# A selective-scan block between two FP4 FFNs: all four channel chunks interleaved in the scan's tiles, and GpSimd making one of four B·du tiles

## The chip, the cores and the metric

The kernel runs on one core of one Trainium2 chip. The metric is the device time of one execution in microseconds (us); shorter is better. A core has five engines that each work through their own instruction queue in order: TensorE (PE: matmuls and transposes; PEld is its weight load), VectorE (DVE), ScalarE (ACT), GpSimd (POOL, which here also issues the accumulating DMAs) and SyncE (SP, which issues the other DMAs). [...] All arithmetic of this kernel is in f32.

## The reference, cut to what matters

The input is 8 sequences of 1024 tokens with 256 features. It passes through `x + 0.5 FFN(norm(x))`, then `x + Mamba(norm(x))`, then the same FFN again. Each FFN quantizes its activations and weights to FP4 in blocks of 16 and multiplies by 256x704, 256x704 and 704x256 matrices. The part that the change touches is the selective scan: 512 channels d, 16 states n, and for each batch a recurrence over the tokens t.

```python
dA = jnp.exp(delta[..., None] * A[None, None])
dBu = delta[..., None] * Bm[:, :, None, :] * u[..., None]
def step(h, inp):
    dA_t, dBu_t, c_t = inp
    h = dA_t * h + dBu_t
    y = jnp.einsum('bdn,bn->bd', h, c_t)
...
y = y + u * D_param          # then  y * silu(z) @ out_proj_w
```

## The kernel before

The 8192 tokens are cut into 16 chunks of 512 tokens (two per sequence). Every chunk s passes through five generators, `stage_f1` (first FFN), `stage_m1` (in-projection, convolution, x-projection, delta, du), `stage_z` (the gate), `scan` and `stage_out` (gate product, out-projection, second FFN). A table of due times at the end of the kernel lets the generators of several chunks emit their instructions interleaved, so that while chunk s is scanned, its neighbours' FFNs and projections run on the same engines.

For the scan the 512 channels are four channel chunks dc of 128 partitions, and the tokens lie along the free dimension. For each of the 16 states k, `scan_step` does four things:

- ACT multiplies `duT` (tokens on partitions, four token tiles t of 128 tokens by 512 channels) by the column of B for state k, which is one scalar per partition: four tiles `s_bu` of 128x512 (line 874). Line 872 could give some of them to DVE, but `BE` is zero, so all are ACT's. There are 7 buffers for these tiles.
- PE transposes each `s_bu` tile in four 128x128 blocks into the PSUM tile `s_pb`, so that channels are on partitions again (line 881). There are two `s_pb` buffers.
- ACT makes `s_da = exp(A delta)`, 128x512, for each dc (line 878).
- DVE runs the recurrence, one scan of 512 tokens for each dc (line 883), from `s_da` and `s_pb` into the tile `h`.

A tile `h` holds one state of all 512 channels, 2048 values on each of 128 partitions, in 5 buffers that are shared with `m_ud` and some prologue tiles. Its layout is `pairs`: two halves a, in each the tokens t, and at each token the two channel chunks q of the pair lie side by side. So a scan writes every second value, and half a is complete after the second of its two scans. `times_c` (line 888) then multiplies each half by the row of C on GpSimd, 1024 values with each value of C used for two neighbours. ACT copies the last token's state to `s_carry` when the sequence has a second chunk (line 908); the multiplication overwrites `h`, so the second half waits for this copy too. Then GpSimd issues one DMA that adds the whole tile to one of two accumulators `accd` in HBM (line 920); SP stores the first one of the odd states (line 918), and `stage_m1` stores u·D there first (`m_ud`, lines 802 to 804). After the last state two more DMAs bring both accumulators back into `h` (lines 914, 915), and `stage_out` multiplies with the gate `m_sz`, again on GpSimd, in two halves (line 852). In the last chunk (s = 15) DVE takes part in the last two multiplications and in the sum.

The order of the instructions on each engine is not the order of the program. `set_order` builds the graph of all instructions, prices each by `price` (lines 141 to 177), plans forwards and backwards many times, plays the best plans with random delays and pins the best order for each engine. The prices that matter here are for GpSimd:

```python
if kind == "InstTensorTensor":
    step, inner = dims(ins[1])[-1]
    return n * (2.106 if step else 1.64 + 0.47 / inner) + (165 if n > 16 else 145), 0, 0, port
if kind == "InstTensorScalarPtr":
    slow = sum(size(a) == 1 for a in ins) > 1
    return (n * 4 + 190 if slow else n + 330), 0, 0, port
```

Whatever changes an instruction or its price therefore changes the order on all engines. GpSimd has other work that is ordered around the scan: the scale and the two block-wise multiplications of the FP4 quantization (lines 543, 545, 552), two small operations of each layer norm (610, 613), and delta·u (803).

Of the kernel before, what the change touches and what calls it, by code (L numbers as in the profile page):

```python
# [11 lines left out]
F32 = mybir.dt.float32  # L12
BF16 = mybir.dt.bfloat16
I32 = mybir.dt.int32
AF = mybir.ActivationFunctionType
ALU = mybir.AluOpType
# [5 lines left out]
P = 128  # L22
T = 512
# [14 lines left out]
KS = 1  # L38
KE = 1
W_T = ((0.01, 0.08, 0.085), (0.02, 0.09, 0.095), (0.15, 0.25, 0.3), 0.2)  # L40

BE = (0,)
CE = (0,)
BUFS = {
    'accd': 4, 'bcol': 2, 'big': 1, 'bu': 7, 'carry': 2, 'cbc': 2, 'cd': 4, 'da': 4, 'delta': 2,
# [17 lines left out]
ND = DI // P  # L63
# [364 lines left out]
def macaron(ctx: ExitStack, tc: tile.TileContext, x_in, norm_w, norm_b, in_w, conv_w,  # L428
            conv_b, xp_w, dt_w, dt_b, a_log, d_par, out_w, w_gate, w_up, w_down, out):
    nc = tc.nc  # L430
    NB, L, _ = x_in.shape
    chunks = []
    for b in range(NB):
        t = 0
# [3 lines left out]
    S = len(chunks)  # L438

    const = ctx.enter_context(tc.tile_pool(name="const", bufs=1))  # L440
    sb = ctx.enter_context(tc.tile_pool(name="sb", bufs=2))
# [16 lines left out]
    dr = ctx.enter_context(tc.tile_pool(name="dr", bufs=3, space=DRAM))  # L458
    sb, psq, psb, dr = Pool(sb), Pool(psq), Pool(psb), Pool(dr)
    pools = [Pool(q) for q in pools]  # L460

    def pst(shape, name):
        turn[kind[0]] += 1
        i = PSM[kind[0]][turn[kind[0]] % len(PSM[kind[0]])]
        t = pools[i].tile([P, 512], F32, tag=f"ps{i}", name=name)
        n = 1
        for k in shape[1:]:
            n *= k
        v = t[: shape[0], :n]
        if len(shape) == 3:  # L470
            v = v.rearrange("p (a b) -> p a b", a=shape[1])
        return v
# [14 lines left out]
    def cload(shape, src, name):  # L487
        t = const.tile(shape, F32, name=name)
        loads.append((t, src))
        return t  # L490
# [3 lines left out]
    def eng(what):  # L494
        return getattr(nc, ENG[what])
# [15 lines left out]
    dh = cload([P, ND], d_par.rearrange("(c p) -> p c", p=P), "dh")  # L511
# [14 lines left out]
        nc.vector.tensor_scalar(an, an, -1.0, None, ALU.mult)  # L526
        yield

    def pairs(h, n):

        return h.rearrange("p (a t q) -> p a t q", a=ND // 2, q=2)[:, :, :n, :]


    def quant(v, n, floor, mul0, mul1):
# [162 lines left out]
    x1d, accd, szd, cd = {}, {}, {}, {}  # L697
    duT, delta, bcol = {}, {}, {}
    carry = {}
# [3 lines left out]
    def tok(ap, s):  # L703
        b, t0, n = chunks[s]
        return ap[b, t0 : t0 + n, :].rearrange("(t p) d -> p t d", p=P)
# [11 lines left out]
    def stage_m1(s):  # L717
        n = chunks[s][2]
        nt = n // P
# [14 lines left out]
        for pr in range(nt // 2):  # L734
# [4 lines left out]
            for j in range(2):  # L739
                t = 2 * pr + j  # L740
                b, r = stats[t]
# [8 lines left out]
        u2 = sb.tile([P, ND, T], F32, tag="big", bufs=BUFS["big"], name="m_u2")  # L750
# [29 lines left out]
        pb = pst([P, nt, P], "m_pb")  # L780
# [12 lines left out]
        nc.scalar.activation(dl, dl, AF.Softplus)  # L793
        yield

        accd[s] = dr.tile([2, P, ND // 2, 2 * T], F32, tag="accd", bufs=BUFS["accd"], name="accd")
        ud = pairs(sb.tile([P, ND * T], F32, tag="h", bufs=BUFS["h"], name="m_ud"), n)
        dg = 1 if fine else DG
        for d0 in range(0, ND, dg):
            d1 = slice(d0, d0 + dg)  # L800
            for dc in range(d0, d0 + dg):
                nc.scalar.activation(ud[:, dc // 2, :, dc % 2], u2[:, dc, :n], AF.Copy, scale=dh[:, dc : dc + 1])
            eng('du').tensor_tensor(u2[:, d1, :n], u2[:, d1, :n], dl[:, d1], ALU.mult)
        nc.sync.dma_start(accd[s][0], ud.rearrange("p a t q -> p a (t q)"))
        yield
        duT[s] = []
        for t in range(nt):
# [22 lines left out]
    y_of, last_h = {}, {}  # L830

    def load_y(s):
        y = pairs(sb.tile([P, ND * T], F32, tag="big", bufs=BUFS["big"], name="o_y"), chunks[s][2])
        yf = y.rearrange("p a t q -> p a (t q)")
        nc.sync.dma_start(yf, accd[s][0])
        nc.gpsimd.dma_start(yf, accd[s][1], accum_op=ALU.add)
        return y

    def stage_out(s):
        n = chunks[s][2]  # L840
        nt = n // P
        muls = (eng('hx'), eng('hq')) if s < S - ENDV else (nc.vector, nc.vector)
        x4 = sb.tile([P, NT, DM], F32, tag="x4", bufs=BUFS["x4"], name="x4b")
        nc.sync.dma_start(x4[:, :nt], x1d[s][:, :nt])
        y, sz = y_of.pop(s), szd[s]

        for a in range(ND // 2):
            if s in last_h:
                for h in last_h[s]:
                    nc.vector.tensor_tensor(y[:, a], y[:, a], h[:, a], ALU.add)  # L850
            zv = sz[:, 2 * a : 2 * a + 2, :]
            (eng('y') if s < S - KE else nc.vector).tensor_tensor(zv, y[:, a].rearrange("p t q -> p q t"), zv, ALU.mult)
        yield
        for t in range(nt):
            po = pst([P, DM], "o_po")
            for dc in range(ND):
                nc.tensor.matmul(po, sz[:, dc, t * P : (t + 1) * P], outw[:, dc, :], start=(dc == 0), stop=(dc == ND - 1))  # L857
            nc.vector.tensor_tensor(x4[:, t, :], x4[:, t, :], po, ALU.add)
        yield
        yield from ffn(x4, nt, muls, s >= S - KE)  # L860
        nc.sync.dma_start(tok(out, s), x4[:, :nt])

    def scan_step(s, k, h):
        n = chunks[s][2]
        nt = n // P
        first = chunks[s][1] == 0
        bu_v = BE[S - 1 - s] if S - 1 - s < len(BE) else 0
        bu = []
        for t in range(nt):
            b = sb.tile([P, DI], F32, tag="bu", bufs=BUFS["bu"], name="s_bu")  # L870
            if t * bu_v % nt < bu_v:
                nc.vector.tensor_scalar(b, duT[s][t], bcol[s][:, t, k : k + 1], None, ALU.mult)
            else:
                nc.scalar.activation(b, duT[s][t], AF.Copy, scale=bcol[s][:, t, k : k + 1])  # L874
            bu.append(b)
        for dc in range(ND):
            da = sb.tile([P, T], F32, tag="da", bufs=BUFS["da"], name="s_da")[:, :n]
            nc.scalar.activation(da, delta[s][dc], AF.Exp, scale=an[:, dc, k : k + 1])  # L878
            pb = psb.tile([P, T], F32, tag="psb", name="s_pb")[:, :n]
            for t in range(nt):  # L880
                nc.tensor.transpose(pb[:, t * P : (t + 1) * P], bu[t][:, dc * P : (dc + 1) * P], ident)  # L881
            init = 0.0 if first else carry[chunks[s][0]][:, k, dc : dc + 1]
            nc.vector.tensor_tensor_scan(h[:, dc // 2, :, dc % 2], da, pb, init, ALU.mult, ALU.add)  # L883

    def times_c(s, k, h, cbc):
        last = s >= S - KE and k >= NS - 2
        for a in range(ND // 2):
            (nc.vector if last and a else nc.gpsimd).tensor_tensor(  # L888
                h[:, a], h[:, a], cbc.unsqueeze(2).to_broadcast([P, chunks[s][2], 2]), ALU.mult)

    def scan(s):
        n = chunks[s][2]
        if chunks[s][1] == 0:

            carry[chunks[s][0]] = sb.tile([P, NS, ND], F32, tag="carry", bufs=BUFS["carry"], name="s_carry")
        for k in range(0, NS, 2):
            cbc = sb.tile([P, 2, T], F32, tag="cbc", bufs=BUFS["cbc"], name="s_cbc")[:, :, :n]
            nc.sync.dma_start(cbc, cd[s][0:1, k * n : (k + 2) * n].rearrange("o (a t) -> o a t", a=2)
                              .partition_broadcast(P))
            if s >= S - KE and k == NS - 2:  # L900
                y_of[s] = load_y(s)
            last = s >= S - KE and k == NS - 2
            for j in range(2):
                h = pairs(sb.tile([P, ND * T], F32, tag="h", bufs=BUFS["h"], name="s_h"), n)
                hf = h.rearrange("p a t q -> p a (t q)")
                scan_step(s, k + j, h)
                if chunks[s][1] + n < L:
                    nc.scalar.activation(carry[chunks[s][0]][:, k + j].rearrange("p (a q) -> p a q", q=2), h[:, :, n - 1, :], AF.Copy)  # L908
                times_c(s, k + j, h, cbc[:, j, :])
                if last:  # L910
                    last_h.setdefault(s, []).append(h)
                elif k + j == NS - 1:

                    nc.gpsimd.dma_start(hf, accd[s][1], accum_op=ALU.add)
                    nc.gpsimd.dma_start(hf, accd[s][0], accum_op=ALU.add)
                    y_of[s] = h
                elif k + j == 1:
                    nc.sync.dma_start(accd[s][1], hf)
                else:
                    nc.gpsimd.dma_start(accd[s][j], hf, accum_op=ALU.add)  # L920
                yield


# [55 lines left out]
```

## Time and profile before

| | |
|---|---|
| time, median of 3 runs | 2452.26 us (2449.67 to 2452.42) |
| profiled execution, its own time | 2451.14 us |
| span of its trace | 2449.0 us |
| PE busy | 2341.7 us (96%) |
| DVE busy | 2177.9 us (89%) |
| ACT busy | 2142.2 us (87%) |
| POOL busy | 2064.2 us (84%) |
| DMA | 416.28 MB, 170 GB/s over the span |

Busy time of an engine is the time covered by its instructions; idle time is given with the event that ended it. A group of instructions is named by line, engine, operation and tiles, with its number, its busy time and the mean duration of one. A view of windows gives the busy time of each engine in a stretch of the span, counted from its start, with the number of instructions in brackets, then the granted TensorE clock (1.00 is full), the mean busy share of the DMA engines, and the rate. A row on POOL that follows a DMA issue can start before the issue's row has ended, so means of such rows are somewhat long.

### The profile page before, as it was taken

The page shows a single profiled execution, that of the slowest core. Times are in us where ns is not written, and L with a number is a line of the kernel's source. Part 1 is how long each engine was busy: PE and PEld are TensorE (multiplying, and loading weights), DVE is VectorE, ACT ScalarE, POOL GpSimd, SP SyncE. Part 2 cuts the span into 40 slices and gives each one's busy share as a digit, 9 for nine tenths or more (in the row PEclk, how much of TensorE's full clock was granted, in tenths as well). Part 3 has the DMA queues.
Part 4 walks back from the last instruction along what each step waited for, and adds up shares of the span by engine and source line. Part 5 has one row for each costly group of instructions (what it writes and reads, how often), then busy time and mean ns, then how long its engine had stood idle before and what let it go on. Part 6 is the DMA issues. An engine that isn't in the chain of part 4 may idle for free.

```text
span 2449.0 us, 33713 instructions
## 1 busy us (share of the span) xinstructions
PE 2341.7 (96%) x11260; PEld 1617.9 (66%) x11260; DVE 2177.9 (89%) x3074; ACT 2142.2 (87%) x3952; POOL 2064.2 (84%) x1554
## 2 busy tenths in 40 slices
PE   7989999999999999999999999999999999998888
PEld 5566666667676666666667666666667666655556
DVE  7569898998989899898999889898998989888995
ACT  4489898999989998998999899898998999999852
POOL 4358898899989999898897999899898999888972
PEclk8999999999999999999999999999999999999899
DMA  3049888787877888598886978889787888899970
GB/s 94 18 115 192 192 166 197 166 200 170 165 191 168 203 185 187 138 185 193 175 196 140 210 169 171 189 173 208 167 178 174 179 190 191 189 211 199 198 149 18
DMA packets 90461, 416.28 MB, mean 170 GB/s; under 512 B 12016, under 2 KB 30320, under 8 KB 53552
## 3 DMA queue, kind: packets, MB, share of 16 engines
q0 software_dynamic: 36576, 266.35, 57.6%
q1 hardware_dynamic: 53712, 147.78, 18.4%
q8 instruction: 88, 1.44, 0.2%
q14 instruction: 85, 0.70, 0.1%
HBM read 129.42 MB, written 284.69 MB: 169 GB/s over the span
## 4 chain that ended last, share of the span: by engine, by line
PE 59%; ACT 13%; POOL 11%; DVE 8%; issue 4%; DMA 3%; SPq 0%; POOLq 0%; DVEq 0%; ACTq 0%
PE s_pb L881 11%; PE f_po L662 9%; PE f_pg L642 9%; PE f_pu L642 8%; PE m_pc L765 6%; POOL s_h L888 5%; DVE s_h L883 4%; ACT s_bu L874 4%; PE m_px L755 3%; ACT s_da L878 3%; PE m_pz L823 3%; PE o_po L857 2%; PE m_pp L775 2%; PE m_pd L791 2%; DMA s_h<-accd 2%
## 5 line engine op out<-in xcount | busy, mean ns | idle before, releaser
L888 POOL TENSOR_TENSOR s_h<-s_h,s_cbc 128x1024 f32<-128x1024 f32 x510 | 1136.9, 2270 | 125.0 <-ACT s_carry L908 71.0
L878 ACT ACTIVATE s_da<-m_delta,an 128x512 f32<-128x512 f32 x1024 | 720.7, 718 | 35.3 <-DVE s_h L883 33.5
L881 PEld LDWEIGHTS s_pb<-ident,s_bu 128*128 128x128 f32 x4096 | 505.3, 142 | 335.6 <-issue 132.5
L874 ACT ACTIVATE s_bu<-m_duT,m_bc 128x512 f32<-128x512 f32 x1024 | 701.4, 717 | 12.5 <-PE s_pb L881 9.9
L881 PE MATMUL s_pb<-ident,s_bu 128*128 128x128 f32 x4096 | 652.3, 277 | 44.7 <-DVE s_h L883 34.4
L883 DVE TENSOR_TENSOR_SCAN s_h<-s_da,s_carry,s_pb 128x512 f32<-128x512 f32 x512 | 638.3, 1264 | 22.2 <-PE s_pb L881 18.9
L883 DVE TENSOR_TENSOR_SCAN s_h<-s_da,s_pb 128x512 f32<-128x512 f32 x512 | 608.5, 1206 | 27.3 <-PE s_pb L881 20.2
L662 PE MATMUL f_po<-wdn,f_ht 128*128 128x256 f32 x1536 | 395.3, 382 | 10.0 <-ACT f_ht L659 7.8
L642 PE MATMUL f_pg<-wg,f_xt 128*128 128x352 f32 x1024 | 365.4, 465 | 4.4 <-ACT f_xt L632 1.8
L642 PE MATMUL f_pu<-wu,f_xt 128*128 128x352 f32 x1024 | 360.3, 463 | 5.2 <-DVE f_h L646 3.2
L662 PEld LDWEIGHTS f_po<-wdn,f_ht 128*128 128x128 f32 x1536 | 270.0, 190 | 76.2 <-issue 22.7
L765 PE MATMUL m_pc<-m_xp,cdg 128*128 128x512 f32 x512 | 253.4, 596 | 1.9 <-ACT m_car L762 1.8
L552 POOL TENSOR_TENSOR f_h<-f_h,q_sc 128x704 f32<-128x704 f32 x128 | 195.9, 1534 | 50.8 <-DVE f_h L551 46.2
L642 PEld LDWEIGHTS f_pu<-wu,f_xt 128*128 128x128 f32 x1024 | 177.6, 191 | 89.5 <-issue 21.7
L920 POOL DMA_DIRECT2D accd<-s_h x223 | 209.6, 940 | 26.3 <-POOL s_h L888 18.0
L642 PEld LDWEIGHTS f_pg<-wg,f_xt 128*128 128x128 f32 x1024 | 176.0, 191 | 80.7 <-issue 21.1
L545 POOL TENSOR_TENSOR f_h<-f_h,q_rc 128x704 f32<-128x704 f32 x120 | 176.5, 1479 | 17.0 <-DVE q_rc L544 10.3
L646 DVE SCALAR_TENSOR_TENSOR f_h<-f_h,f_pg 128x352 f32<-128x352 f32 x256 | 129.0, 505 | 37.6 <-ACT f_h L645 36.5
L645 ACT ACTIVATE f_h<-f_pg 128x352 f32<-128x352 f32 x256 | 116.9, 457 | 48.0 <-PE f_pg L642 47.5
L543 POOL TENSOR_SCALAR q_sc<-q_mx 128x44 f32<-128x44 f32 (+2 forms) x198 | 85.5, 439 | 74.2 <-DVE q_mx L542 66.8
L647 DVE TENSOR_TENSOR f_h<-f_h,f_pu 128x352 f32<-128x352 f32 x256 | 129.3, 506 | 18.7 <-PE f_pu L642 17.2
L755 PE MATMUL m_px<-m_hnT,inw 128*128 128x512 f32 x256 | 128.0, 606 | 3.0 <-DVE m_u L769 1.7
(114 smaller groups left out, 3384.6 us busy)
## 6 DMA issues: line engine op xcount, KB each, us to landing
accd<-s_h POOLq DMA_DIRECT2D x223, 1024.0 KB, 9.6
s_cbc<-cd SPq DMA_DIRECT2D x128, 512.0 KB, 6.0
s_h<-accd POOLq DMA_DIRECT2D x30, 1024.0 KB, 8.5
accd<-m_ud SPq DMA_DIRECT2D x16, 1024.0 KB, 13.1
accd<-s_h SPq DMA_DIRECT2D x16, 1024.0 KB, 5.8
x4a<-_attn_hidden_states_dram SPq DMA_DIRECT2D x16, 512.0 KB, 4.3
x1d<-x4a SPq DMA_DIRECT2D x16, 512.0 KB, 6.5
x4b<-x1d SPq DMA_DIRECT2D x16, 512.0 KB, 3.5
```

Source lines behind the costliest of these rows:

```text
L545: mul0.tensor_tensor(vb, vb, rc.unsqueeze(2).to_broadcast([P, g, BLK]), ALU.mult)
L552: mul1.tensor_tensor(vb, vb, sc.unsqueeze(2).to_broadcast([P, g, BLK]), ALU.mult)
L642: nc.tensor.matmul(dst, xt[:, c, :], w[:, c, hf * FH : (hf + 1) * FH], start=(c == 0), stop=(c == 1))
L662: nc.tensor.matmul(po, ht[:, k, :], wdn[:, k, :], start=(k == 0), stop=(k == NF - 1))
L755: nc.tensor.matmul(px, inw[:, c, dc * P : (dc + 1) * P], hnT[:, c, :n], start=(c == 0), stop=(c == 1))
L765: nc.tensor.matmul(pc, cdg[:, dc, k, :], xp[:, k : k + n], start=(k == 0), stop=(k == KC - 1))
L874: nc.scalar.activation(b, duT[s][t], AF.Copy, scale=bcol[s][:, t, k : k + 1])
L878: nc.scalar.activation(da, delta[s][dc], AF.Exp, scale=an[:, dc, k : k + 1])
L881: nc.tensor.transpose(pb[:, t * P : (t + 1) * P], bu[t][:, dc * P : (dc + 1) * P], ident)
L883: nc.vector.tensor_tensor_scan(h[:, dc // 2, :, dc % 2], da, pb, init, ALU.mult, ALU.add)
L888: (nc.vector if last and a else nc.gpsimd).tensor_tensor(h[:, a], h[:, a], cbc.unsqueeze(2).to_broadcast([P, chunks[s][2], 2]), ALU.mult)
L920: nc.gpsimd.dma_start(accd[s][j], hf, accum_op=ALU.add)
```

## The change

The layout of `h`, `m_ud` and `o_y` becomes `mixed`: at each token the values of all four channel chunks lie side by side, so a scan writes every fourth value. The halves of `times_c` and of the gate product are now the first and the last 256 tokens, each with all four channel chunks; each value of C serves four neighbours. The accumulators' DMAs move the same flat 2048 values per partition. In all chunks but the last, the first token tile (t = 0) of `s_bu` of each of the 16 states is made by GpSimd instead of ACT: 15 x 16 = 240 tiles.

```diff
-BE = (0,)
-CE = (0,)
+BP = tuple((k, 0) for k in range(16))
...
-    def pairs(h, n):
-        return h.rearrange("p (a t q) -> p a t q", a=ND // 2, q=2)[:, :, :n, :]
+    def mixed(h, n):
+        return h.rearrange("p (t q) -> p t q", q=ND)[:, :n, :]
+    def flat(h):
+        return h.rearrange("p t q -> p (t q)")
+    def halves(n):
+        return [slice(0, n // 2), slice(n // 2, n)] if n == T else [slice(0, n)]
...
-                nc.scalar.activation(ud[:, dc // 2, :, dc % 2], u2[:, dc, :n], AF.Copy, scale=dh[:, dc : dc + 1])
+                nc.scalar.activation(ud[:, :, dc], u2[:, dc, :n], AF.Copy, scale=dh[:, dc : dc + 1])
...
-        for a in range(ND // 2):
+        for a in halves(n):
             if s in last_h:
                 for h in last_h[s]:
                     nc.vector.tensor_tensor(y[:, a], y[:, a], h[:, a], ALU.add)
-            zv = sz[:, 2 * a : 2 * a + 2, :]
+            zv = sz[:, :, a]
             (eng('y') if s < S - KE else nc.vector).tensor_tensor(zv, y[:, a].rearrange("p t q -> p q t"), zv, ALU.mult)
...
-            if t * bu_v % nt < bu_v:
-                nc.vector.tensor_scalar(b, duT[s][t], bcol[s][:, t, k : k + 1], None, ALU.mult)
+            if s < S - KE and (k, t) in BP:
+                nc.gpsimd.tensor_scalar(b, duT[s][t], bcol[s][:, t, k : k + 1], None, ALU.mult)
...
-            nc.vector.tensor_tensor_scan(h[:, dc // 2, :, dc % 2], da, pb, init, ALU.mult, ALU.add)
+            nc.vector.tensor_tensor_scan(h[:, :, dc], da, pb, init, ALU.mult, ALU.add)
...
-        for a in range(ND // 2):
-            (nc.vector if last and a else nc.gpsimd).tensor_tensor(
-                h[:, a], h[:, a], cbc.unsqueeze(2).to_broadcast([P, chunks[s][2], 2]), ALU.mult)
+        for a in halves(chunks[s][2]):
+            m = a.stop - a.start
+            (nc.vector if last and not a.start else nc.gpsimd).tensor_tensor(
+                h[:, a], h[:, a], cbc[:, a].unsqueeze(2).to_broadcast([P, m, ND]), ALU.mult)
...
-                    nc.scalar.activation(carry[chunks[s][0]][:, k + j].rearrange("p (a q) -> p a q", q=2), h[:, :, n - 1, :], AF.Copy)
+                    nc.scalar.activation(carry[chunks[s][0]][:, k + j], h[:, n - 1, :], AF.Copy)
```

More of the change, by code (lines that the diff above doesn't have):

```diff
@@ L794, in stage_m1 @@
         yield
-        accd[s] = dr.tile([2, P, ND // 2, 2 * T], F32, tag="accd", bufs=BUFS["accd"], name="accd")
-        ud = pairs(sb.tile([P, ND * T], F32, tag="h", bufs=BUFS["h"], name="m_ud"), n)
+        accd[s] = dr.tile([2, P, ND * T], F32, tag="accd", bufs=BUFS["accd"], name="accd")
+        ud = mixed(sb.tile([P, ND * T], F32, tag="h", bufs=BUFS["h"], name="m_ud"), n)
         dg = 1 if fine else DG
@@ L801, in stage_m1 @@
             for dc in range(d0, d0 + dg):
-                nc.scalar.activation(ud[:, dc // 2, :, dc % 2], u2[:, dc, :n], AF.Copy, scale=dh[:, dc : dc + 1])
+                nc.scalar.activation(ud[:, :, dc], u2[:, dc, :n], AF.Copy, scale=dh[:, dc : dc + 1])
             eng('du').tensor_tensor(u2[:, d1, :n], u2[:, d1, :n], dl[:, d1], ALU.mult)
-        nc.sync.dma_start(accd[s][0], ud.rearrange("p a t q -> p a (t q)"))
+        nc.sync.dma_start(accd[s][0, :, : ND * n], flat(ud))
         yield
@@ L832, in load_y @@
     def load_y(s):
[L833 to L836, printed above, removed]
+        n = chunks[s][2]
+        y = mixed(sb.tile([P, ND * T], F32, tag="big", bufs=BUFS["big"], name="o_y"), n)
+        nc.sync.dma_start(flat(y), accd[s][0, :, : ND * n])
+        nc.gpsimd.dma_start(flat(y), accd[s][1, :, : ND * n], accum_op=ALU.add)
         return y
@@ L866, in scan_step @@
         first = chunks[s][1] == 0
-        bu_v = BE[S - 1 - s] if S - 1 - s < len(BE) else 0
         bu = []
@@ L903, in scan @@
             for j in range(2):
-                h = pairs(sb.tile([P, ND * T], F32, tag="h", bufs=BUFS["h"], name="s_h"), n)
-                hf = h.rearrange("p a t q -> p a (t q)")
+                h = mixed(sb.tile([P, ND * T], F32, tag="h", bufs=BUFS["h"], name="s_h"), n)
                 scan_step(s, k + j, h)
                 if chunks[s][1] + n < L:
-                    nc.scalar.activation(carry[chunks[s][0]][:, k + j].rearrange("p (a q) -> p a q", q=2), h[:, :, n - 1, :], AF.Copy)
+                    nc.scalar.activation(carry[chunks[s][0]][:, k + j], h[:, n - 1, :], AF.Copy)
                 times_c(s, k + j, h, cbc[:, j, :])
@@ L912, in scan @@
                 elif k + j == NS - 1:
-                    nc.gpsimd.dma_start(hf, accd[s][1], accum_op=ALU.add)
-                    nc.gpsimd.dma_start(hf, accd[s][0], accum_op=ALU.add)
+                    nc.gpsimd.dma_start(flat(h), accd[s][1, :, : ND * n], accum_op=ALU.add)
+                    nc.gpsimd.dma_start(flat(h), accd[s][0, :, : ND * n], accum_op=ALU.add)
                     y_of[s] = h
                 elif k + j == 1:
-                    nc.sync.dma_start(accd[s][1], hf)
+                    nc.sync.dma_start(accd[s][1, :, : ND * n], flat(h))
                 else:
-                    nc.gpsimd.dma_start(accd[s][j], hf, accum_op=ALU.add)
+                    nc.gpsimd.dma_start(accd[s][j, :, : ND * n], flat(h), accum_op=ALU.add)
                 yield
```

## The prediction

> **What bounds the kernel now.** I read the page's busy shares first, then the busy time in six stretches of 300 us away from both ends, then finer windows, and last the groups of the lines that change. The stretches from 300 to 2100 us:
>
> ```profile
> 300.00:600.00 300.00, 295.88 (x1454) 207.67 (x1453) 279.71 (x397) 280.37 (x520) 271.53 (x204) 1.00 0.82 183
> 600.00:900.00 300.00, 294.82 (x1427) 202.85 (x1427) 281.08 (x398) 278.63 (x515) 274.12 (x204) 1.00 0.82 182
> 900.00:1200.00 300.00, 294.19 (x1420) 202.89 (x1419) 275.41 (x391) 274.70 (x506) 267.78 (x199) 0.99 0.82 179
> 1200.00:1500.00 300.00, 293.15 (x1413) 202.56 (x1412) 275.07 (x394) 273.38 (x504) 265.89 (x200) 1.00 0.80 178
> 1500.00:1800.00 300.00, 295.04 (x1434) 204.71 (x1433) 278.78 (x399) 276.13 (x513) 270.39 (x204) 1.00 0.80 178
> 1800.00:2100.00 300.00, 297.52 (x1451) 206.67 (x1449) 281.71 (x389) 280.36 (x517) 273.85 (x201) 1.00 0.82 182
> ```
>
> The columns are PE, PEld, DVE, ACT, POOL. Over these 1800 us PE is busy 1770.6 us (98.4%), DVE 1671.8 (92.9%), ACT 1663.6 (92.4%), POOL 1623.6 (90.2%). PE bounds, but three engines stand close behind. The page counts 11260 matmuls; less 280 that keep the clock up and 36 for the weights, that is 684 for each of 16 chunks, and the 8599 in these stretches are 12.57 chunks: 143.2 us each. Per chunk PE works 140.9, DVE 133.0, ACT 132.3, POOL 129.2 us. At most 2.3 us per chunk, 35 us in all, can be won without less PE work, and the change takes none away.
>
> The average hides phases. Over 38 windows of 24 us from 880 to 1792 us, PE is busy 892.52 of 912 us, 23.49 each. Four of the worse ones:
>
> ```profile
> 1024.00:1048.00 24.00, 22.27 (x108) 14.84 (x107) 23.89 (x33) 24.00 (x49) 21.75 (x15) 1.00 0.61 129
> ...
> 1360.00:1384.00 24.00, 22.34 (x109) 14.82 (x108) 20.84 (x28) 22.30 (x44) 23.84 (x22) 1.00 0.82 163
> ...
> 1408.00:1432.00 24.00, 21.93 (x108) 14.89 (x106) 18.17 (x33) 19.09 (x32) 23.53 (x19) 1.00 0.78 169
> ...
> 1744.00:1768.00 24.00, 22.14 (x102) 13.98 (x101) 23.21 (x29) 24.00 (x46) 23.22 (x18) 1.00 0.82 200
> ```
>
> PE loses time where ACT is full (first and last line) and where POOL is full (the two between). In the 7 windows with ACT at 23.6 us or more PE averages 22.97; in the 6 with POOL at 23.5 or more it averages 22.77, 0.72 below the mean. These are the two engines that the change trades against each other.
>
> **The change part by part.** The groups that carry the prices:
>
> ```profile
> L888 POOL TENSOR_TENSOR s_h<-s_h,s_cbc 128x1024 f32<-128x1024 f32 x510 | 1136.9, 2270 | 125.0 <-ACT s_carry L908 71.0 <-DVE s_h L883 48.8 <-DMA s_cbc<-cd 2.0
> ...
> L545 POOL TENSOR_TENSOR f_h<-f_h,q_rc 128x704 f32<-128x704 f32 x120 | 176.5, 1479 | 17.0 <-DVE q_rc L544 10.3 <-PE s_pb L881 4.7 <-PE m_pz L823 0.6
> ...
> L803 POOL TENSOR_TENSOR m_u<-m_u,m_delta 128x1024 f32<-128x1024 f32 x30 | 74.0, 2501 | 0.2
> L545 POOL TENSOR_TENSOR f_xn<-f_xn,q_rc 128x512 f32<-128x512 f32 x64 | 73.1, 1142 | 5.4 <-DVE q_rc L544 5.3
> L852 POOL TENSOR_TENSOR m_sz<-s_h,m_sz 128x1024 f32<-128x1024 f32 x30 | 72.5, 2433 | 18.9 <-DMA s_h<-accd 18.1 <-DVE m_sz L827 0.7
> ...
> L503 POOL MEMSET dtw<- 64x512 f32 x1 | 0.5, 523 | 0.1
> ```
>
> ```profile
> L874 ACT ACTIVATE s_bu<-m_duT,m_bc 128x512 f32<-128x512 f32 x1024 | 701.4, 717 | 12.5 <-PE s_pb L881 9.9
> ```
>
> *ACT loses 240 tiles*, 16 per chunk x 0.717 = 11.5 us: 132.3 becomes 120.8 us per chunk, 84% of the period.
>
> *POOL gains them.* No row shows GpSimd multiplying 512 values by one scalar per partition. Below, it costs at least what writing 512 values costs (523 ns); above, no more than two-operand products of 512 (1142 ns). With one operand read and one written it stands between, and I take the middle, 0.85 us, which is also what the planner will believe (512 + 330 = 842 ns). Per chunk 13.6 us, from 8.4 to 18.3.
>
> *POOL's products with C get cheaper.* With 0.2 us of fixed cost (the 128x2 product of line 613 shows 196 ns), a value costs 2.25 ns where the second operand is read fresh for each (line 803), 2.02 where it serves two (888), 1.82 where it serves 16 (545, 704 values). That is 1.80 + 0.45/r for r neighbours; for r = 4 it gives 1.91, so 2.15 us instead of 2.27. 32 x 0.12 = 3.7 us per chunk; bounds 0 and 32 x 0.21 = 6.7 (the price at 16).
>
> *The gate product* (line 852) now reads `h` at every fourth value, 16 bytes apart. At 8 bytes it costs 2433 ns against 2501 contiguous, so nothing is seen of a stride; on ACT the strided store of `m_ud` costs a median of 765 against 713 ns for `s_bu`. I take 0 to 7% of 2.43 us, twice per chunk: 0 to 0.3 us.
>
> [...]
>
> *The scan's store and `m_ud`'s* go from 8 to 16 bytes too. The scan takes 1206 and 1264 ns for 512 values, about twice a DVE product per value (1218 ns for 1024), so its store has time; I take 0, and 52 ns as the upper end, from ACT's strided store: 64 x 0.052 = 3.3 us of DVE per chunk, 136.3 of 143.2, still covered. If the cover were gone, it would be 50 us. `m_ud` at most doubles that small surcharge, 0.2 us of ACT per chunk, covered by the 11.5 us freed.
>
> *Waits.* Both halves of a product now wait for the fourth scan; before, the first half went after the second. What is queued behind it on POOL is the quantization's products and now the next states' `s_bu`, for which PE waits. In exchange, the copy of the last token touches only the second half, so the 71.0 us for which POOL waited for `s_carry` go; what is late next is the fourth scan (48.8 us now). A tile `h` is held about two products longer (2.3 us); five buffers at one state per 8.95 us give 45 us, against some 9 us of scans, 4.5 of products and 9.6 us for the DMA to land, so nothing waits there. The DMAs issue as before, same number and size, but behind 16 more POOL instructions per chunk; SP's queue is unchanged.
>
> *The ends.* In the last chunk GpSimd makes no `s_bu`. Its last product waits two scans more (under 1 us lost, since DVE does the other half), and the out-projection of the first 256 tokens can start after one half's sums and product, 3 x 1.22 us sooner. I count -2 us.
>
> **The sum.** POOL per chunk: 129.2 + 13.6 - 3.7 + 0.1 = 139.2 us, 97% of 143.2 (from 130.9 to 147.8 with all bounds, 91 to 103%). In a window of 24 us that is 1.66 us more. Then all windows that now have 21.84 or more are full: 16 of 38 instead of 6. Ten more at 0.72 us is 7.2 us in 912, and over 15 chunks (2148 us) +17 us. What doesn't fit into full windows, 12.9 us in 912, has room in the emptier ones (17.29 us at 1000 to 1024); I let a sixth stick, +5. ACT's full windows get their loss back, 7 x 0.52 us in 912: -9. With -2 for the end, 2451.1 + 17 + 5 - 9 - 2 = 2462 us on the profiled execution's own time; the median lies 1 us above it: 2463 us, 0.4% slower. A new order on every engine comes on top, with no row to price it.
>
> **The rivals.**
> *POOL stays hidden, and ACT's relief decides (faster).* For it: POOL's products feed a DMA and not PE, so it may lag by many microseconds; PE waits now for ACT and DVE (`s_pb` for `s_bu`, and for the scans, which wait for `s_da`), and ACT is at 24.00 of 24 in several windows. Against it: POOL also quantizes for the FFN, and now makes the first operand of every transpose group. Decides if the new tile costs under some 0.65 us, where POOL stays below 95%. PE could go from 98.4 to 99.2%: 1.2 us x 15 = -17, ends -2 and the start -4 (ACT 111 of 120 us busy from 180 to 300): 2428 to 2445.
> *POOL becomes the bound.* At 1.14 us a tile POOL needs 143.8 us per chunk; at the 98.4% that the fullest engine reaches now this is 146.1, +2.9 x 15 = +44: 2496. With the upper ends of the stride and no cheaper product it is 147.8/0.984 = 150.2, +105: 2557. For it: POOL already has windows of 23.8 of 24. Against it: one operand should be cheaper than two.
> *Nothing moves.* PE's 140.9 us is the floor and both effects cancel: 2447 to 2457.
> *The swap misses its aim:* ACT is relieved, but PE now waits for POOL instead, through the same two `s_pb` buffers; the time is that of the sum above.
>
> **How the numbers follow.** POOL full, slightly slower (2457 to 2490): 0.45; POOL bound (2490 to 2560): 0.14; hidden (2425 to 2447): 0.30; nothing: 0.11. So faster 0.30, same 0.11, slower 0.59, with 0.2% as about what a measurement can tell. The likeliest case alone spans 2457 to 2490. The range reaches from 2428 (the hidden case's best) to 2532, between the two prices of the bound case, which leaves out some 0.05 below and 0.1 above.
>
> **What would show it.** Right: GpSimd's new group of 240 at 0.8 to 0.9 us; line 888 at about 2.15 us; ACT near 84% and POOL near 97% in the middle; POOL's wait for `s_carry` gone; PE's waits for `s_bu` naming POOL. Wrong: a new group above 1.1 us or below 0.65, scans longer than 1264 ns, a gate product above 3 us, or PE rising above 98.4% in the middle, which would mean that POOL's load is hidden after all.

## The result, and the profile after

The changed kernel takes 2617.85 us (median of 4 runs, 2616.29 to 2622.96) against 2451.39 us before (also 4 runs, one more than in the table above): a ratio of 1.0683, 95% interval 1.0665 to 1.0702. It is 166 us slower. I had forecast 2463 us, slower by 0.4%, in a range up to 2532 us.

The page of the changed kernel, busy time and then the engines' shares of the chain that ended last:

```profile
PE 2386.6 (91%) x11260; PEld 1625.3 (62%) x11260; DVE 2191.5 (84%) x3074; ACT 2044.1 (78%) x3712; POOL 2386.0 (91%) x1794
...
POOL 50%; PE 21%; issue 11%; DVE 8%; ACT 7%; DMA 3%; SPq 0%; POOLq 0%; ACTq 0%; DVEq 0%
```

Before, the same line of the chain began with

```profile
PE 59%; ACT 13%; POOL 11%; DVE 8%; issue 4%; DMA 3%; SPq 0%; POOLq 0%; DVEq 0%; ACTq 0%
```

The bound has moved from PE to GpSimd. The windows of 300 us of the changed kernel say the same (columns PE, PEld, DVE, ACT, POOL, then clock, DMA share, GB/s):

```profile
300.00:600.00 300.00, 280.61 (x1327) 190.58 (x1328) 260.66 (x379) 244.94 (x447) 293.11 (x221) 0.99 0.76 165
600.00:900.00 300.00, 281.41 (x1342) 190.79 (x1341) 262.43 (x372) 245.08 (x445) 295.49 (x219) 0.99 0.76 167
...
1500.00:1800.00 300.00, 280.37 (x1337) 191.18 (x1336) 261.71 (x370) 244.06 (x449) 295.15 (x222) 0.99 0.76 165
```

From 300 to 2100 us POOL is busy 97.8%, PE 93.4, DVE 86.8, ACT 81.4. The 7974 matmuls in this stretch are, at 684 per chunk, 11.66 chunks: 154.4 us each instead of 143.2. The 11.2 us more, over 15 chunks, are 168 us: by this the whole loss is here and not at the ends. POOL works 151.0 us per chunk, before 129.2. The granted TensorE clock is 0.99 in all six stretches, against 0.99 to 1.00 before, so a lower clock is not what costs 7%. The groups that carry it:

```profile
L892 POOL TENSOR_TENSOR s_h<-s_h,s_cbc 128x1024 f32<-128x1024 f32 x510 | 1147.7, 2371 | 25.3 <-DVE s_h L886 19.2 <-ACT m_delta L797 3.1 <-ACT s_carry L911 1.6
...
L886 DVE TENSOR_TENSOR_SCAN s_h<-s_da,s_carry,s_pb 128x512 f32<-128x512 f32 x512 | 643.9, 1267 | 27.5 <-PE s_pb L884 19.8 <-ACT f_xt L636 4.2 <-ACT s_da L881 1.0
...
L877 ACT ACTIVATE s_bu<-m_duT,m_bc 128x512 f32<-128x512 f32 x784 | 539.5, 713 | 24.5 <-PE s_pb L884 22.3 <-POOL s_h L892 1.0
L875 POOL TENSOR_SCALAR s_bu<-m_duT,m_bc 128x512 f32<-128x512 f32 x240 | 455.1, 1896 | 12.6 <-PE s_pb L884 11.2 <-ACT m_duT L816 0.2
...
L856 POOL TENSOR_TENSOR m_sz<-s_h,m_sz 128x1024 f32<-128x1024 f32 x30 | 93.9, 3168 | 2.7 <-DMA s_h<-accd 2.6
...
L806 ACT ACTIVATE m_ud<-m_u,dh 128x512 f32<-128x512 f32 x64 | 77.0, 1234 | 1.1 <-DVE m_u L773 1.1
```

The new group (line 875) takes 1896 ns on average where I had put 850. In the list of waits of the changed kernel the largest that name an engine are still for VectorE's scans; ACT's for them is the first line below, and it was 33.5 us before. The waits that name POOL are mostly not in the scan but in the quantization, whose instructions share POOL's queue with the tiles (who waited, for whom, us in total, times, longest):

```profile
ACT s_da L881 <- DVE s_h L886: 122.5, 157, 3.1
...
DVE q_rc L548 <- POOL q_sc L547: 91.3, 88, 3.9
ACT q_q L553 <- POOL f_h L549: 78.2, 58, 3.9
...
ACT f_xn L628 <- POOL bn_nm L617: 40.6, 24, 3.5
PEld f_pt L634 <- POOL f_xn L556: 39.2, 38, 3.3
...
PEld s_pb L884 <- POOL s_bu L875: 11.3, 14, 2.2
```

A row on POOL can be too long here. In the timeline (start, us, engine, line), cut to rows of POOL, a tile that follows a product takes 1.56 us. Behind a DMA issue a row begins before the last has ended, and this goes on through the rows that follow without a pause:

```profile
1603.49 1.56 POOL L875 TENSOR_SCALAR s_bu<-m_duT,m_bc 128x512 f32<-128x512 f32 x1
...
1608.01 0.87 POOL L923 DMA_DIRECT2D accd<-s_h  x1
...
1608.67 2.27 POOL L892 TENSOR_TENSOR s_h<-s_h,s_cbc 128x1024 f32<-128x1024 f32 x1
...
1610.65 1.63 POOL L556 TENSOR_TENSOR f_h<-f_h,q_sc 128x704 f32<-128x704 f32 x1
```

Where POOL is full, its busy time per chunk, which counts no stretch twice, is therefore the better measure than the mean or the median of a row.

### The profile page after: what moved, and what is told of

It reads as the page before. It is cut to its first block, busy times and chain, and to the rows that moved or that the text cites. A ratio compares the mean times of both kernels' runs of the same rounds, so it can differ in the third digit from the quotient of the medians.

```text
span 2621.2 us, 33872 instructions
## 1 busy us (share of the span) xinstructions
PE 2386.6 (91%) x11260; PEld 1625.3 (62%) x11260; DVE 2191.5 (84%) x3074; ACT 2044.1 (78%) x3712; POOL 2386.0 (91%) x1794
## 4 chain that ended last, share of the span: by engine, by line
POOL 50%; PE 21%; issue 11%; DVE 8%; ACT 7%; DMA 3%; SPq 0%; POOLq 0%; ACTq 0%; DVEq 0%
POOL s_h L892 19%; POOL s_bu L875 8%; POOL accd L923 5%; PE f_po L666 4%; POOL f_h L549 4%; DVE s_h L886 4%; POOL f_h L556 3%; PE s_pb L884 3%; PE f_pg L646 3%; PE f_pu L646 3%; POOL m_sz L856 2%; POOL q_sc L547 2%; POOL f_xn L556 2%; POOL m_u L807 2%; POOL bn_y L614 2%
## 5 line engine op out<-in xcount | busy, mean ns | idle before, releaser
L892 POOL TENSOR_TENSOR s_h<-s_h,s_cbc 128x1024 f32<-128x1024 f32 x510 | 1147.7, 2371 | 25.3 <-DVE s_h L886 19.2
L884 PE MATMUL s_pb<-ident,s_bu 128*128 128x128 f32 x4096 | 666.9, 278 | 83.4 <-DVE s_h L886 68.0
L886 DVE TENSOR_TENSOR_SCAN s_h<-s_da,s_carry,s_pb 128x512 f32<-128x512 f32 x512 | 643.9, 1267 | 27.5 <-PE s_pb L884 19.8
L886 DVE TENSOR_TENSOR_SCAN s_h<-s_da,s_pb 128x512 f32<-128x512 f32 x512 | 613.6, 1211 | 53.6 <-PE s_pb L884 45.3
L877 ACT ACTIVATE s_bu<-m_duT,m_bc 128x512 f32<-128x512 f32 x784 | 539.5, 713 | 24.5 <-PE s_pb L884 22.3
L875 POOL TENSOR_SCALAR s_bu<-m_duT,m_bc 128x512 f32<-128x512 f32 x240 | 455.1, 1896 | 12.6 <-PE s_pb L884 11.2
L666 PE MATMUL f_po<-wdn,f_ht 128*128 128x256 f32 x1536 | 405.1, 389 | 23.1 <-ACT f_ht L659 13.9
L923 POOL DMA_DIRECT2D accd<-s_h x223 | 250.8, 1125 | 10.9 <-POOL s_h L892 6.7
L556 POOL TENSOR_TENSOR f_h<-f_h,q_sc 128x704 f32<-128x704 f32 x128 | 215.1, 1680 | 41.7 <-DVE f_h L555 41.5
L646 PEld LDWEIGHTS f_pg<-wg,f_xt 128*128 128x128 f32 x1024 | 178.8, 192 | 96.9 <-issue 22.6
L549 POOL TENSOR_TENSOR f_h<-f_h,q_rc 128x704 f32<-128x704 f32 x120 | 208.8, 1740 | 6.3 <-DVE q_rc L548 4.8
L547 POOL TENSOR_SCALAR q_sc<-q_mx 128x44 f32<-128x44 f32 (+2 forms) x198 | 123.4, 623 | 63.0 <-DVE q_mx L546 55.3
L553 ACT ACTIVATE q_q<-f_h 128x704 f32<-128x704 f32 x128 | 97.2, 760 | 89.9 <-POOL f_h L549 78.2
```

Of the source, the lines that this page charges most:

```text
L549: mul0.tensor_tensor(vb, vb, rc.unsqueeze(2).to_broadcast([P, g, BLK]), ALU.mult)
L556: mul1.tensor_tensor(vb, vb, sc.unsqueeze(2).to_broadcast([P, g, BLK]), ALU.mult)
L646: nc.tensor.matmul(dst, xt[:, c, :], w[:, c, hf * FH : (hf + 1) * FH], start=(c == 0), stop=(c == 1))
L666: nc.tensor.matmul(po, ht[:, k, :], wdn[:, k, :], start=(k == 0), stop=(k == NF - 1))
L875: nc.gpsimd.tensor_scalar(b, duT[s][t], bcol[s][:, t, k : k + 1], None, ALU.mult)
L886: nc.vector.tensor_tensor_scan(h[:, :, dc], da, pb, init, ALU.mult, ALU.add)
```

## The experiments

The theories: **load** (the tiles are long, POOL's work per chunk exceeds what the period allows), **layout** (the later start of the products and the wider strides), and **order** (the planner prices a tile at 842 ns and builds an order that doesn't hold). POOL's work per chunk is counted in all runs as above, from the windows between 300 and 2100 us.

**1. The layout alone.** All tiles back on ACT.

```diff
-BP = tuple((k, 0) for k in range(16))
+BP = ()
```

> The changed kernel with all token tiles on ACT again; only the layout of four channel chunks side by side is left. Load theory (the 240 tiles on GpSimd, 1.56 us and more each, make POOL the bound): POOL per chunk 129.2 - 32 x 0.13 (products 2.15 to 2.02 us) + 2 x 0.75 (gate products) = 126.5 us, ACT 132.3 + 4 x 0.47 (m_ud) = 134.2 us, PE stays the bound: 2440 to 2465 us. Layout theory (the later start of the products and the 16-byte strides cost the time): above 2530 us, most of the 166 us stays.

2474.61 us, ratio 1.0084 (1.0068 to 1.0101): 23 us of the 166, 10 us more than the load theory allowed and far from the layout theory. POOL works 126.2 us per chunk, as worked out (126.5). The first halves now wait for the fourth scan, 143.3 us in all instead of 48.8, and the wait for `s_carry` shrinks from 71.0 to 9.6 us:

```profile
L892 POOL TENSOR_TENSOR s_h<-s_h,s_cbc 128x1024 f32<-128x1024 f32 x510 | 1067.0, 2147 | 166.9 <-DVE s_h L886 143.3 <-ACT s_carry L911 9.6 <-DVE bn_mv L612 5.7
```

**2. The tiles alone.** The old layout, with GpSimd making the 240 tiles.

```diff
-            if t * bu_v % nt < bu_v:
-                nc.vector.tensor_scalar(b, duT[s][t], bcol[s][:, t, k : k + 1], None, ALU.mult)
+            if s < S - KE and t == 0:
+                nc.gpsimd.tensor_scalar(b, duT[s][t], bcol[s][:, t, k : k + 1], None, ALU.mult)
```

> The kernel before, in its old layout, with the first token tile of every state on GpSimd in all chunks but the last. Load theory: POOL per chunk 129.2 + 16 x 1.56 = 154.2 us; at the 97.8% that POOL reaches in the changed kernel the period is 157.6 us, 14.4 us above 143.2, and 15 chunks give 2451 + 216 = 2667 us (2630 to 2700), slower than the whole change. Layout theory: below 2530 us.

2657.92 us, ratio 1.0840 (1.0824 to 1.0856), as the load theory said, and slower than the whole change: the layout gives POOL some of its time back. POOL works 153.6 us per chunk (worked out 154.2) in a period of 156.5 us.

**3. The right price in the planner.**

```diff
-        return (n * 4 + 190 if slow else n + 330), 0, 0, port
+        one = sum(size(a) == 1 for a in ins) == 1
+        return (n * 4 + 190 if slow else n * 3 + 20 if one else n + 330), 0, 0, port
```

> The changed kernel with one line of the planner changed: a GpSimd product with one scalar per partition is priced at 512 x 3 + 20 = 1556 ns, the shortest measured, in place of 842. The work is the same, only the order can differ. Load theory: POOL still has 151 us per chunk, 2590 to 2625 us. Order theory (the plan was built on a price that is half of the real one, and the wrong order costs the time): below 2540 us.

2592.95 us, ratio 1.0577 (1.0561 to 1.0593). The same 151.0 us of POOL's work per chunk, now with POOL busy 99.1% of the time and a period of 152.4 us. Two of its stretches (columns as above):

```profile
300.00:600.00 300.00, 285.63 (x1320) 191.75 (x1320) 262.46 (x382) 244.15 (x443) 296.70 (x221) 0.98 0.76 166
...
1500.00:1800.00 300.00, 285.69 (x1360) 192.73 (x1360) 264.08 (x374) 249.66 (x453) 298.62 (x224) 1.00 0.77 171
```

So 25 of the 166 us go with this other order. A still better one could win some 21 us more by an estimate (15 chunks of 151.0 instead of 152.4 us); by the same estimate the other 120 us stay as long as POOL has this work.

**4. Another operation for the same tile.** A product of two tensors, the column of B with step 0, planned at its own price.

```diff
-                nc.gpsimd.tensor_scalar(b, duT[s][t], bcol[s][:, t, k : k + 1], None, ALU.mult)
+                nc.gpsimd.tensor_tensor(b, duT[s][t], bcol[s][:, t, k : k + 1].to_broadcast([P, DI]), ALU.mult)
```

> The changed kernel with the 240 tiles made by GpSimd as a product of two tensors, the column of B spread over 512 columns with step 0, in place of the product with a scalar per partition. From the rows of line 545 one costs about 1.05 us instead of 1.56. Load theory: POOL per chunk 151 - 16 x 0.5 = 143 us, at 97.8% a period of 146.2 us, 2451 + 15 x 3 = 2496 us (2470 to 2515). If the number of instructions on POOL and not their length were what counts: 2590 us or more.

2508.49 us, ratio 1.0231 (1.0215 to 1.0246). POOL works 141.6 us per chunk in a period of 146.7 us, 96.6%. As many instructions on POOL as in the change, but 109 us less time, in another order. This speaks for their length; run 5 takes the order out.

**5. The same, with every instruction at its place.** In run 4 the order changed too. Here the operation is that of run 4 and the planner is told that it costs 842 ns; the resulting order is the changed kernel's on all five engines.

```diff
-        step, inner = dims(ins[1])[-1]
+        step, inner = dims(ins[1])[-1] if "s_bu" not in outs[0].bass_ap.tensor.name else (0, 0.47 * 512 / (842 - 165 - 1.64 * 512))
```

> The changed kernel with every instruction at its place in the order of each engine; only the operation of the 240 tiles is another, a product of two tensors with step 0 (1.04 us undisturbed) in place of a product with a scalar per partition (1.57 us). The planner is told the same 842 ns. Load theory: POOL per chunk 151 - 16 x 0.53 = 142.5 us, at 97.8% a period of 145.7 us, about 2489 us (2480 to 2515): nearly all of the 166 us goes with the length of this one operation. Order theory (the plan on a price that is too low is what costs): above 2560 us.

2527.14 us, ratio 1.0310 (1.0285 to 1.0336). Only the operation differs from the changed kernel, and 91 of the 166 us are gone: that much is shown as the price of this one operation. It misses my range by 12 us: POOL's 141.8 us of work per chunk take a period of 147.6 us, 96.1%, and the 97.8% of the formula is not reached. The tile of this run (min, median and max duration, first and last start):

```profile
L875 POOL TENSOR_TENSOR s_bu<-m_duT,m_bc x240: 1030/1302/2120, 144.3 to 2293.3; 128x512 f32<-128x512 f32 x120
```

against that of the changed kernel:

```profile
L875 POOL TENSOR_SCALAR s_bu<-m_duT,m_bc x240: 1552/1838/2737, 144.0 to 2392.2; 128x512 f32<-128x512 f32 x120
```

**6. The disputed price by itself.** At the start of the kernel, three GpSimd operations of each kind on a tile that nothing else uses yet. In the order that the planner made they stand among GpSimd's other work of the first 53 us, so a single row of a group can be too long.

```diff
+    for _ in range(3):
+        nc.gpsimd.tensor_scalar(pa[:, :512], pb_[:, 0, :], pc_, None, ALU.mult)
+    ...
```

> The kernel before with 21 GpSimd operations of 128x512 f32 at the very start, three of each kind, before other work is there to disturb them. If a GpSimd product with a scalar costs some 3 ns for each value whatever the scalar is: about 1.55 us with a scalar per partition, 0.8 us for 256 values, 1.55 us with a constant. If the scalar's place in memory is what costs: the constant at about 0.85 us. Products of two tensors: 1.03 us with step 0, 1.08 us with four neighbours, 1.14 us with two; a copy 0.5 to 0.9 us.

The rows, in the order of the program: scalar per partition with 512 and with 256 values, constant with 512, then with 512 values each a product with step 0, a copy, products with four and with two neighbours:

```profile
L486 POOL TENSOR_SCALAR pl<-pl,mhalf x3: 1565/1573/1587, 3.9 to 9.0; 128x512 f32<-128x512 f32 x3
L488 POOL TENSOR_SCALAR pl<-pl,mhalf x3: 925/925/1406, 10.7 to 18.7; 128x256 f32<-128x256 f32 x3
L490 POOL TENSOR_SCALAR pl<-pl x3: 1493/1494/1849, 20.1 to 25.5; 128x512 f32<-128x512 f32 x3
L492 POOL TENSOR_TENSOR pl<-pl,mhalf x3: 1041/1042/1043, 31.3 to 35.5; 128x512 f32<-128x512 f32 x3
L494 POOL COPY pl<-pl x3: 611/1152/1269, 36.6 to 42.1; 128x512 f32<-128x512 f32 x3
L496 POOL TENSOR_TENSOR pl<-pl x3: 1092/1101/1425, 42.8 to 46.7; 128x512 f32<-128x512 f32 x3
L498 POOL TENSOR_TENSOR pl<-pl x3: 1154/1159/1162, 49.1 to 51.5; 128x512 f32<-128x512 f32 x3
```

A product with a scalar costs 1573 ns for 512 values and 925 for 256: 2.5 ns for each value and 0.28 us fixed. Where the scalar comes from hardly matters (1494 ns with a constant). The product of two tensors, which reads more, costs 1042 ns. The three rows of the copy differ too much (611 to 1269 ns) to give a price. (The kernel took 2495 us in its one run, with this work at its start and another order; nothing is read from that time.)

**7. The strides.** The layout alone, in the same order on all engines as in run 1, but `m_ud` written and `h` read for the gate product without a stride; the channels then stand at other places in these two operations. The first edit makes the planner take every part of `m_ud` for the whole tile, which keeps the order of run 1.

```diff
-    return t.name, off, off + sum(s * (k - 1) for s, k in d)
+    return (t.name, 0, 2047) if "m_ud" in t.name else (t.name, off, off + sum(s * (k - 1) for s, k in d))
...
-                nc.scalar.activation(ud[:, :, dc], u2[:, dc, :n], AF.Copy, scale=dh[:, dc : dc + 1])
+                nc.scalar.activation(flat(ud)[:, dc * n : (dc + 1) * n], u2[:, dc, :n], AF.Copy, scale=dh[:, dc : dc + 1])
...
-            ... y[:, a].rearrange("p t q -> p q t") ...
+            ... flat(y[:, a]).rearrange("p (q t) -> p q t", q=ND) ...
```

> The layout alone, as in the run of that name, with the same order of instructions on all five engines, but the two accesses that went from a stride of 8 to one of 16 bytes outside the scan are contiguous: m_ud is written, and the gate product reads h, without a stride. This leaves the right placing of the channels out of these two operations, so the output isn't the reference's; count and size of all instructions stay. Stride theory (64 m_ud of 1.24 us instead of 0.77, 30 gate products of 3.06 instead of 2.43 us cost the 23 us of the layout): m_ud below 0.77, gate products at 2.4 to 2.5 us, and 2450 to 2460 us in all. Late-start theory (the products begin two scans later): 2468 to 2480 us as before.

2462.92 us, ratio 1.0047 (1.0032 to 1.0062), between the two expectations: 12 of the layout's 23 us go with the strides, 11 stay. The rows of run 1 and, below them, of this run:

```profile
L806 ACT ACTIVATE m_ud<-m_u,dh x64: 1195/1241/1277, 93.5 to 2249.2; 128x512 f32<-128x512 f32 x64
```

```profile
L806 ACT ACTIVATE m_ud<-m_u,dh x64: 705/712/735, 93.5 to 2234.6; 128x512 f32<-128x512 f32 x64
```

The gate products on GpSimd in the kernel before, in run 1 and in this run:

```profile
L852 POOL TENSOR_TENSOR m_sz<-s_h,m_sz x30: 2405/2421/2617, 288.3 to 2277.9; 128x1024 f32<-128x1024 f32 x30
```

```profile
L856 POOL TENSOR_TENSOR m_sz<-s_h,m_sz x30: 2870/2949/3522, 300.8 to 2297.6; 128x1024 f32<-128x1024 f32 x30
```

```profile
L856 POOL TENSOR_TENSOR m_sz<-s_h,m_sz x30: 2359/2394/2959, 300.8 to 2282.1; 128x1024 f32<-128x1024 f32 x30
```

Which of the two accesses costs the 12 us was not tried. In the stretch from 300 to 2100 us this run executes 8598 matmuls, the kernel before 8599: a period of 143.2 us in both. So the 11 us that stay are lost before and behind that stretch, and there the later start of the products costs nothing that can be seen.

**8 to 10. What another order is worth.** Three runs ask how much of a small difference is the planner's pick. The kernel before with other random delays in the play:

```diff
-    ... g.play(u, random.Random(k)) ...
+    ... g.play(u, random.Random(k + 200)) ...
```

> The kernel before with other random delays in the play that picks among the planned orders; another of the planner's orders is picked, the work is the same. If picks are worth little: within 0.3% of before, 2444 to 2459 us. If picks differ by 0.8% and more (above 2470 or below 2432 us), the 23 us of the layout can't be told from the planner's luck.

2465.07 us, ratio 1.0054 (1.0039 to 1.0069). The kernel before with other starting weights:

```diff
-WEIGHTS = (0.05, 0.1, 0.15, 0.2, 0.3)
+WEIGHTS = (0.06, 0.12, 0.17, 0.22, 0.35)
```

> The kernel before with the planner's five starting weights moved a little (0.06, 0.12, 0.17, 0.22, 0.35); the work is the same, the order another. A second sample of the planner's luck: 2445 to 2470 us if the 13 us of the first one are typical; within 5 us of before if that one was an outlier.

2481.12 us, ratio 1.0118 (1.0103 to 1.0133): some 29 us for nothing but another order, more than I had expected. Run 7 with the other delays:

> The layout alone with the two strided accesses contiguous, with other random delays in the play that picks the order. Its first pick took 2463 us. If the 11 us that were left over before are the planner's luck: anywhere from 2445 to 2475 us. If the late start of the products costs them: 2460 us or more. Output isn't the reference's, since channels stand at wrong places in m_ud and in the gate product.

2460.57 us, ratio 1.0037 (1.0026 to 1.0049). Both other orders of the kernel before are slower than its own, so a kernel that is planned anew may lose some 29 us by its order alone; two samples give no bound. The 11 us that run 7 leaves over are inside that. Whether they come from the order or from the late start of the products at both ends of the kernel stays open.

**11 and 12. A few tiles, to relieve ACT where it is full.** The old layout, with the first token tile of the first four states made by GpSimd (as a product, the edit below) or by VectorE (the condition alone, its first two lines).

```diff
-            if t * bu_v % nt < bu_v:
+            if s < S - KE and t == 0 and k < 4:
-                nc.vector.tensor_scalar(b, duT[s][t], bcol[s][:, t, k : k + 1], None, ALU.mult)
+                nc.gpsimd.tensor_tensor(b, duT[s][t], bcol[s][:, t, k : k + 1].to_broadcast([P, DI]), ALU.mult)
```

> The kernel before in its old layout; in all chunks but the last GpSimd makes the first token tile of the first four states only, as a product with the column of B spread with step 0. POOL per chunk 129.2 + 4 x 1.05 = 133.4 us (93% of 143.2), ACT 132.3 - 2.9 = 129.4 us, and the relief falls where ACT was full (the first states of a chunk). Relief theory: 2430 to 2446 us. Tight theory (anything on POOL costs, since PE waits for what stands behind it): 2452 to 2465 us.

> The kernel before in its old layout; in all chunks but the last VectorE makes the first token tile of the first four states. ACT 129.4 us per chunk as in the run with four tiles on GpSimd, POOL untouched at 129.2, DVE 133.0 + 4 x 0.4 = 134.6. If ACT's relief is worth something by itself: 2432 to 2446 us. If PE was not held by ACT: 2449 to 2470 us, within the planner's picks.

2478.89 us (ratio 1.0109, 1.0092 to 1.0126) and 2485.22 us (1.0130, 1.0112 to 1.0148). Both lie above all that I had expected of them. Neither gains, and the loss is about that of another order (run of the weights: 2481 us), so it can't be put down to the tiles. On VectorE a tile took a median of 502 ns and up to 2682, not the 400 planned. No version here beats the kernel before.

## Why the prediction was wrong, point by point

- **What bounds before: right.** PE at 98.4%, with three engines close behind; POOL was the engine that a small addition could fill.
- **The new tile, "I take the middle, 0.85 us", bounds 523 to 1142 ns: wrong, and the step that failed.** It costs 1573 ns undisturbed, outside both bounds, and the sign that I had set for this, a group above 1.1 us, is there. The upper bound rested on "one operand should be cheaper than two", read from products of two tensors of the same size. On GpSimd these are different operations with different prices for each value, 2.5 ns against an estimated 1.6 to 1.8 (1042 and 1142 ns less the 0.2 us fixed). The planner's 842 ns, which I put beside it, is a guess in the kernel's own code and no evidence. The trace of before did show a relative of the operation, only smaller: the quantization's scale is a `tensor_scalar` too, though with two steps, times 1/6 and then no less than a floor. Two of its sizes stand undisturbed in the timeline (start, us, engine, line):

```profile
1204.51 0.36 POOL L543 TENSOR_SCALAR q_sc<-q_mx 128x44 f32<-128x44 f32 x1 [0.25 <-DVE q_mx L542]
...
1208.12 0.32 POOL L543 TENSOR_SCALAR q_sc<-q_mx 128x32 f32<-128x32 f32 x1
```

  Twelve values more cost 0.04 us, 3.3 ns each; carried to 512 values that is 0.32 + 480 x 0.0033 = 1.9 us. A rough extrapolation from an operation that does more, but it would have put the upper end beyond the truth.
- **POOL's sum: right but for that term and, smaller, the gate product.** With measured prices it is 129.2 + 16 x 1.57 - 32 x 0.12 + 2 x 0.53 = 151.5 us per chunk; measured 151.0. The rival in which POOL becomes the bound has the mechanism and the formula: 151.5/0.984 = 154.0, 10.8 us more in each of 15 chunks, 2613 us against 2618 measured. I had given it 0.14, with its top at 2557, since the price of a tile was bounded at 1.14 us there too.
- **The cheaper products: right.** 2.27 to 2.15 us expected on average, 2270 to 2147 ns measured in the layout alone (medians 2147 and 2024). In the whole change the rows read longer (a mean of 2371), because there more of them begin before the row ahead has ended; POOL's 151.0 us per chunk agree with the shorter price.
- **The strides: mixed.** The scan's store is free, as taken (1267 and 1211 ns against 1264 and 1206). The store of `m_ud` has a median of 1241 ns in the layout alone instead of 765, a surcharge over `s_bu` of 528 ns, where I had let the 52 ns at most double. The gate product was priced at 0 to 7% more and costs 22% (2949 against 2421 ns, medians in the layout alone; in the whole change its mean, 3168 ns, passes the 3 us that I had set as a sign of being wrong).
- **The waits: right on POOL, in part behind it.** The 71.0 us for `s_carry` are 1.6 after the change; what is late next is the fourth scan where POOL has time (143.3 us in the layout alone), and little where POOL is full (19.2 us). Of the work that I had named as queued behind, the others wait for the quantization (91.3 and 78.2 us in its two largest waits) and hardly for `s_bu` (11.3 us of PE's weight loads), so the rival in which PE waits for POOL through the `s_pb` buffers is not what is seen.
- **The step from load to time: too kind even for a right load.** With the tile as a product POOL has 141.6 us of work in the old period of 143.2, and the kernel takes 2508 us; dividing by 0.984 would have given 2462. POOL is no fuller than 96.6% there, with PE at 96.9%. How much of this is another order stays open.
- **"A new order comes on top, with no row to price it": true, and it belonged into the sum.** Other orders of unchanged work cost some 13 and 29 us.
- **The ends, "I count -2 us": not seen.** With the strides gone (run 7) the middle is as fast as before and the kernel still takes 11 us longer, so the ends are slower there and not faster; the cause is open.

The 166 us in one chain of runs: the layout +23 (12 of it the strides, shown at an equal order); the 240 tiles as products +34; the same work in the order planned on 842 ns +19; the product with a scalar in place of the product of tensors, at an equal order, +91. The +91 and the 12 us of the strides are shown at an equal order. The +19 is the price of an order by itself. How the +34 divides between POOL's load and another order is not shown; it is of the size that another order alone can make, and so are the other 11 us of the layout.

## What to carry to other kernels

Price a moved operation by a row of that very operation on the engine that receives it, at two sizes if the trace has only small ones, and not by a row of the right size from another operation; when no such row is there, the bound must stay open on the upper side. On an engine that is already busy for 90% of the bounding engine's period, that one term can decide the outcome: here each 0.1 us per tile is 1.6 us per chunk and at most 24 us in all, and the 0.53 us between the two operations cost 91 us, 17 for each 0.1. Where a planner orders the work anew at each change, hold the order fixed to compare two operations, or measure what another order of the same work costs before crediting a percent to an edit.

## What the hardware showed that I had not expected

- GpSimd multiplies 512 values per partition by a scalar in 1573 ns, and by a second tensor with step 0 in 1042 ns. The operation with one more tensor to read is the faster one, by a third.
- ACT's store of 512 values at a stride of 16 bytes takes 1241 ns, contiguous 712, at 8 bytes 765; VectorE's scan stores at 16 bytes as fast as at 8 (1267 and 1264 ns).
- Reading at a stride of 16 bytes is not free for VectorE: its two gate products of the last chunk, 1024 values with `o_y` read at that stride, take 2019 and 2468 ns in the whole change, 1218 and 1221 at 8 bytes (the kernel before) and 1212 and 1226 contiguous (run 7).
- The same work in another order costs up to 1.2% on this kernel (2481 against 2453 us), with every engine's busy time per chunk within 0.4 us of that before; the period is 144.7 instead of 143.2 us.
